# Group statistics of an attention block by VectorE transposes in place of matmuls, one early input block, and a new load order

## The chip, the cores and the metric

The kernel runs on one core of a Trainium2 chip. The metric is the time of one execution on the device in microseconds (us). Several executions are timed, and the median is given with the lowest and the highest. An execution over 1.5% above the fastest of its kernel would count as slow and none was: over all calls the kernel before runs from 1662.96 to 1671.88 us, 0.5% apart (the two single looks, at the kernel before and at the last experiment, count as unknown), and all ratios come from rounds in which the kernel before ran on the same chip.

## The reference

```python
def reference(x, gn_scale, gn_bias, qkv_w, qkv_b, proj_w, proj_b):   # x: (4, 512, 48, 48) f32
    hn = group_norm(x, 32 groups) * gn_scale + gn_bias     # mean and var over 16 channels x 48 x 48
    qkv = einsum('oc,bchw->bohw', qkv_w, hn) + qkv_b       # 1536 x 512
    q, k, v = split(qkv as float16, 8 heads of 64)
    w = softmax((q * s)^T (k * s))                         # 2304 x 2304 for each head and batch
    a = (w v^T) as float32
    return x + einsum('oc,bchw->bohw', proj_w, a) + proj_b
```

The group norm is the part that was changed. A group is 16 neighbouring channels, and channels lie on partitions, so the mean and the variance of a group are sums over 16 partitions. Everything else (three projections, scores, exponentials, values, output projection) is unchanged.

## The kernel before

The 512 channels are 4 chunks (`c`) of 128 partitions; the 2304 positions are 5 blocks (`j`) of 512, 512, 512, 512 and 256. Each batch is 4 pairs of heads (`g`) by 5 blocks, so attention runs through 80 blocks in all. The kernel issues scores and values of one unit after another and puts the projections ("beside" work: q and k as `pqk`, v as `pv`, the output as `pr`) between them, so that TensorE is filled while ScalarE computes exponentials. A block of 512 is six units, one of 256 three; a unit with nothing beside it is called bare. The sums of a softmax row (`sums`) go out and come back by DMA; their inverses come back the same way (`ib`), and GpSimd multiplies by them (the "division", `att`), checks that the sums lie within limits (`in`, `fine`) and converts the attention output to f32 for the output projection (`a`). At a hand-over the next batch's x is loaded, its statistics are taken, and the output projection of the batch before is done.

Statistics and coefficients, with the sum over 16 partitions as a matmul with a constant matrix `gmat2`:

```python
    def group_mean(b, bank, chunks=ALL):
        ...
        nc.tensor.matmul(pm, gmat2, mv[:, :, 0], start=True, stop=True)
        nc.vector.tensor_copy(mean, pm)
        nc.vector.tensor_tensor(dev, mv[:, :, 0], mean, ALU.subtract)
        nc.vector.tensor_tensor(dev2, dev, dev, ALU.mult)
        nc.vector.tensor_tensor(var, mv[:, :, 1], dev2, ALU.add)

    def group_rstd(b, bank, chunks=ALL):
        ...
        nc.tensor.matmul(pv, gmat2, var, start=True, stop=True)
        nc.vector.tensor_scalar(veps, pv, EPS, None, ALU.add)
        nc.gpsimd.tensor_tensor(rstd, veps, mhalf[:, : len(chunks)], ALU.pow)

    def coefficients(b, chunks=ALL):
        ...
        nc.vector.tensor_tensor(ga, rstd, gsc[:, cs], ALU.mult)
        nc.vector.tensor_tensor(mga, mean, ga, ALU.mult)
        nc.vector.tensor_tensor(gb, gbi[:, cs], mga, ALU.subtract)
```

The order at the start, and the residual loads, which the argument below turns on:

```python
    all_stats(0); group_mean(0, ..., (0,)); group_rstd(0, ..., (0,)); all_stats(1)
    for c in range(NC):
        coefficients(0, (c,))
        norm_chunk(0, c)                      # on ScalarE
        if c + 2 < NC: all_stats(c + 2)
        ...                                   # six projections of chunk c; mean and rstd of c + 1 between them
    # (cut) the output projection: x is loaded a second time as the residual r, one tile ahead
        for k, (jj, chunks) in enumerate(proj_list):
            ...
                [piece(0.0, lambda k=k: ahead(k)) for k in ([0] if k == 0 else [])]
                + [piece(0.0, lambda k=k: ahead(k + 1))]
                + ...
```

The first residual tile of a batch is thus loaded when its first output chain is issued, and not sooner. It goes through the same queue of SyncE as the x blocks of the next batch, behind what stands there before it: in the trace of the changed kernel shown below, x loads are issued at 1058.35, the `ib` loads at 1062.01 after a wait of 1.7 us, and the residual at 1063.17.

## Time and profile before

| | before |
|---|---|
| time, median of the first 3 executions | 1666.96 us (1666.34 to 1669.79) |
| span of the profiled execution | 1659.0 us |
| TensorE busy | 1597.6 us, 96% |
| VectorE, ScalarE, GpSimd busy | 68%, 75%, 22% |

The prediction below shows the busy table, the slices, the start and the first hand-over. Beside them stands the table by stretches, here for the three hand-overs and the last batch (columns: stretch; its length; busy time of TensorE, of its weight loads, of VectorE, ScalarE and GpSimd, each with a count; mean granted TensorE clock; DMA share; GB/s):

```profile
250.00:400.00 150.00, 140.68 (x1110) 61.57 (x1108) 120.73 (x149) 122.62 (x130) 36.82 (x41) 0.99 0.17 45
600.00:800.00 200.00, 193.98 (x1424) 93.62 (x1421) 152.02 (x184) 152.88 (x162) 55.20 (x71) 0.99 0.28 80
1000.00:1200.00 200.00, 193.69 (x1436) 92.97 (x1434) 152.04 (x184) 150.85 (x159) 51.17 (x70) 1.00 0.29 81
1400.00:1600.00 200.00, 190.90 (x1328) 88.38 (x1325) 138.28 (x139) 162.82 (x173) 63.34 (x80) 1.00 0.26 75
```

Length less the first busy number is TensorE's idle time: 9.3, 6.0, 6.3 and 9.1 us. Two waits of the output projection, in the table of waits (total us, times, longest us), come back later:

```profile
PE pr L819 <- POOL a L813: 10.8, 13, 1.5
...
PE pr L819 <- DVE r L839: 3.3, 3, 2.7
```

"pr for a" is the wait for GpSimd's conversion of the attention output to f32. "pr for r" is the wait for a free PSUM bank, which VectorE empties by adding the residual r; when r has not landed, VectorE stands and so does TensorE.

### The profile page before, as it was taken

Reading aid. Unit: us, or ns where it says so; the run is one execution under the profiler, and the core shown is the slowest. Engines: PE = TensorE matmul, PEld = TensorE weight load, DVE = VectorE, ACT = ScalarE, POOL = GpSimd, SP = SyncE. Lnnn points to the kernel's source line nnn. Section 1 sums busy time; section 2 is a strip of 40 time slices with the busy share of each in tenths; the row PEclk is TensorE's granted clock in tenths of the full one; section 3 lists DMA queues with packets and bytes.
Section 4 is the critical chain, followed back from the end, with each engine's and each line's share of the span. In section 5 each row is a group of like instructions: output and inputs, shape, how many; then the busy total and the mean of one; then the engine's idle time right before and its main releaser. Section 6 shows DMA issues by size and latency. Waiting matters only on the chain.

```text
span 1659.0 us, 28335 instructions
## 1 busy us (share of the span) xinstructions
PE 1597.6 (96%) x11528; PEld 699.7 (42%) x11528; DVE 1131.3 (68%) x1282; ACT 1246.5 (75%) x1317; POOL 370.8 (22%) x499
## 2 busy tenths in 40 slices
PE   6999999899999999999999999999999999999987
PEld 2533444244333443445433344345533334434445
DVE  4257667887666667878666666887766677676664
ACT  3078788887878877777778777876778888887772
POOL 1002112222121213232111121223111222214241
PEclk9999999999999999999999999999999999999999
DMA  6000002200000002540100000443110000003443
GB/s 215 1 1 23 15 15 65 74 14 17 14 11 14 18 14 60 161 133 17 33 14 11 14 14 11 130 119 112 24 26 11 14 17 15 15 11 124 134 126 120
DMA packets 95184, 82.10 MB, mean 49 GB/s; under 512 B 51140, under 2 KB 61252, under 8 KB 95044
## 3 DMA queue, kind: packets, MB, share of 16 engines
q1 hardware_dynamic: 93572, 79.14, 17.0%
q8 instruction: 92, 1.51, 0.4%
q10 hardware_dynamic: 1344, 1.05, 0.2%
q14 instruction: 48, 0.39, 0.1%
q0 software_dynamic: 128, 0.01, 0.0%
HBM read 60.70 MB, written 19.17 MB: 48 GB/s over the span
## 4 chain that ended last, share of the span: by engine, by line
PE 87%; DVE 4%; DMA 3%; POOL 3%; ACT 2%; issue 1%; SPq 0%; ACTq 0%; DVEq 0%; POOLq 0%
PE pqk L696 28%; PE ps L892 17%; PE av L917 17%; PE pv L741 15%; PE pr L819 7%; POOL a L813 2%; ACT p L899 2%; DVE acc L950 2%; PE ps L696 1%; PE sl L970 1%; DMA row<-inv 1%; DVE acc L953 1%; DMA ib<-row 1%; DMA out_dram<-r 1%; DVE st L605 0%
## 5 line engine op out<-in xcount | busy, mean ns | idle before, releaser
L899 ACT ACTIVATE p<-ps 128x1024 f16<-128x1024 f32 x1296 | 1231.6, 1027 | 360.9 <-PE ps L892 358.4
L950 DVE TENSOR_TENSOR acc<-acc,p 128x3072 f16<-128x3072 f16 x270 | 486.4, 1802 | 69.7 <-ACT p L899 69.0
L696 PE MATMUL pqk<-x,wqkv 128*64 128x512 f32 (+1 forms) x2464 | 518.6, 551 | 0.5 <-DVE k L705 0.4
L892 PE MATMUL ps<-q,k 64*128 64x512 f16 (+1 forms) x2880 | 362.3, 358 | 17.0 <-ACT p L899 14.9
L917 PE MATMUL av<-p,v 128*64 128x512 f16 (+1 forms) x2880 | 361.3, 364 | 0.0
L1008 POOL TENSOR_SCALAR in<-sums 128x8 f32<-128x8 f32 (+1 forms) x160 | 109.7, 686 | 726.3 <-DMA sums<-slx 719.5
L741 PE MATMUL pv<-wqkv,x 128*64 128x256 f32 x2304 | 268.1, 380 | 0.0
L696 PEld LDWEIGHTS pqk<-x,wqkv 128*64 128x64 f32 x2464 | 168.7, 137 | 226.5 <-issue 170.6
L1034 POOL TENSOR_TENSOR att<-avx,ib 128x512 f16<-128x512 f32 (+1 forms) x78 | 132.8, 1703 | 447.0 <-DMA ib<-row 366.1
L892 PEld LDWEIGHTS <-k 64*128 64x128 f16 x2880 | 107.3, 94 | 294.9 <-issue 248.2
L917 PEld LDWEIGHTS <-v 128*64 128x64 f16 x2880 | 131.7, 109 | 209.8 <-issue 165.8
L741 PEld LDWEIGHTS pv<-wqkv,x 128*64 128x64 f32 x2304 | 160.7, 137 | 92.1 <-DVE v L749 5.4
L819 PE MATMUL pr<-a,whi 128*128 128x512 f32 (+1 forms) x320 | 126.5, 403 | 14.0 <-POOL a L813 10.8
L950 DVE TENSOR_TENSOR acc<-p,p 128x3072 f16<-128x3072 f16 x79 | 139.1, 1760 | 0.0
L819 PE MATMUL pr<-a,wlo 128*128 128x512 f32 (+1 forms) x320 | 117.3, 375 | 0.0
L953 DVE TENSOR_TENSOR acc<-acc 128x1024 f16<-128x1024 f16 x156 | 113.3, 726 | 5.3
L705 DVE TENSOR_SCALAR q<-pqk,bqkv 128x512 f16<-128x512 f32 (+1 forms) x79 | 54.9, 695 | 84.2 <-PE pqk L696 83.7
L749 DVE TENSOR_TENSOR v<-pv,bv 128x512 f16<-128x512 f32 x72 | 49.8, 691 | 89.2 <-PE pv L741 88.6
L705 DVE TENSOR_SCALAR k<-pqk,bqkv 128x512 f16<-128x512 f32 (+1 forms) x75 | 52.2, 696 | 80.9 <-PE pqk L696 80.8
L839 DVE SCALAR_TENSOR_TENSOR r<-pr,bproj,r 128x512 f32<-128x512 f32 (+1 forms) x80 | 54.7, 693 | 63.4 <-PE pr L819 56.2
L926 DVE COPY avx<-av 128x512 f32<-128x512 f32 (+1 forms) x80 | 51.0, 637 | 68.6 <-PE av L917 68.4
L819 PEld LDWEIGHTS pr<-a,whi 128*128 128x128 f32 x320 | 60.5, 189 | 56.5 <-POOL a L813 22.6
(61 smaller groups left out, 467.7 us busy)
## 6 DMA issues: line engine op xcount, KB each, us to landing
r<-x_dram SPq DMA_DIRECT2D x72, 256.0 KB, 2.9
out_dram<-r SPq DMA_DIRECT2D x72, 256.0 KB, 3.0
ib<-row SPq DMA_DIRECT2D x126, 128.0 KB, 3.0
x<-x_dram SPq DMA_DIRECT2D x62, 256.0 KB, 4.5
x<-x_dram SPq DMA_DIRECT2D x16, 128.0 KB, 4.7
sums<-slx SPq DMA_DIRECT2D x128, 2.0 KB, 2.1
ib<-row SPq DMA_DIRECT2D x30, 64.0 KB, 2.8
wqkv<-qkv_wT_dram SPq DMA_DIRECT2D x2, 768.0 KB, 6.9
```

Source lines behind the costliest of these rows:

```text
L696: nc.tensor.matmul(pw[0][lo : lo + D, :n], wqkv[:, c, w0 + lo : w0 + lo + D], hn[b, c, j], start=(c == 0), stop=(c == NC - 1),)
L705: nc.vector.tensor_scalar(qk[g][part][:, o : o + n], pw[0][:, :n], bqkv[:, col : col + 1], SCALE, ALU.add, ALU.mult,)
L741: nc.tensor.matmul(pw[0][lo : lo + D, a, :], hn[b, c, i * P // QB][:, at + lo : at + lo + D], wqkv[:, c, 2 * C + half * C // 2 :][:, : C / ...
L819: nc.tensor.matmul(ps[:, :n], w[:, c, bass.ts(m, P)], at32[b, j][c], start=(c == 0 and i == 0), stop=(c == NC - 1 and i == 1),)
L839: nc.vector.scalar_tensor_tensor(xt[:, i], places[i], bproj[:, m : m + 1], xt[:, i], ALU.add, ALU.add)
L892: nc.tensor.matmul(ps[:, h, a * n : (a + 1) * n], kt[rows, bass.ts(i, P)], qt[rows, o : o + n], start=True, stop=True,)
L899: nc.scalar.activation(pt[:, r], ps, AF.Exp)
L917: nc.tensor.matmul(av[0][lo : lo + D, :n], vv[b, pr // 2][:, i, pr % 2 * P + lo : pr % 2 * P + lo + D], pt[:, r, h, a * n : (a + 1) * n], ...
L950: nc.vector.tensor_tensor(t, before, pt, ALU.add)
L953: nc.vector.tensor_tensor(t[:, 0], t[:, 0], t[:, r], ALU.add)
L1008: nc.gpsimd.tensor_scalar(t, sm, limit, None, op)
L1034: nc.gpsimd.tensor_tensor(atts[g][:, o : o + n], avx.pop((g, j))[:, :n], ibs.pop((g, j))[:, :n], ALU.mult,)
```

## The change

The intent is to take the statistics off TensorE: a VectorE transpose (0.31 us for 128x96 f32 in the trace of the changed kernel), which its code uses by squares of 32x32 with a correct result, turns the per-partition moments so that the 16 channels of a group lie along one row, one aggregation per group merges them, and a second transpose turns the coefficients back. With no round trip over TensorE, coefficients come sooner at the start and at hand-overs. The converted attention output, one tile `a32` so far, becomes four, one for each chunk. One block of the second batch's x is loaded early into buffers that the first batch does not use, and some projections are held back to fill the first hand-over. At the start x is loaded ahead of the k weights. (Cut to its core.)

```diff
-    load_w(1, slice(0, P), nc.scalar)
     for c in range(NC):
         for j in range(NQ):
             load_x(0, j, c, nc.scalar if c == 0 and j % 2 else nc.sync)
         if c == 0:
+            load_w(1, slice(0, P), nc.scalar)
             load_w(0, slice(0, P), nc.scalar)
...
-        nc.tensor.matmul(pm, gmat2, mv[:, :, 0], start=True, stop=True)      # group_mean, group_rstd gone
+    def group_scale(b, chunks=ALL):
+        turned = small_tile(SQ * 3, "turned")
+        nc.vector.transpose(turned.rearrange("p (c s) -> p s c", s=3), moments)
+        grouped = small_tile(NGROUP * 2, "grouped").rearrange("p (g s) -> p g s", s=2)
+        for i in range(NGROUP):
+            nc.vector.bn_aggr(grouped[:, i, :], turned[:, bass.ts(i, GROUP * 3)])
+        veps = small_tile(NGROUP, "veps")
+        nc.vector.tensor_scalar(veps, grouped[:, :, 1], EPS, None, ALU.add)
+        rstd = small_tile(NGROUP, "rstd")
+        nc.gpsimd.tensor_tensor(rstd, veps, mhalf, ALU.pow)
+        ...                                      # copy the means into `both`
     def coefficients(b, chunks=ALL):
+        ...                                      # copy rstd into `both`
+        nc.vector.transpose(cols, both)
...
+    SPARE = (1, 3)                               # batch 1, block 3
+        if (b, j) == SPARE:
+            t = work.tile([P, n], F32, tag=f"a32_{c}", bufs=1, name=name)
...
-                t = work.tile([P, NC, QB], F32R, tag="a32", bufs=1, name=f"a32_{b}_{j}")
+                at32[b, j] = [work.tile([P, QB], F32R, tag=f"a32_{c}", bufs=1, ...)[:, :n]
+                              for c in range(NC)]
...
+                tasks.append((now[0] + 3, lambda: aggregate(b)))   # then group_scale, coefficients,
+                tasks.append((now[0] + 3, lambda: group_scale(b))) # normalize, one after the other
...
+            put_run(reload, *SPARE)              # the early block; v tiles and q, k of block 3 held back
...
     for c in range(NC):
+        for j in range(NQ):
+            if j == 2:
+                coefficients(0, (c,)); norm_chunk(0, c)
+            if c + 1 < NC:
+                stats(0, j, c + 1)
```

More of the change, by code (lines that the diff above doesn't have):

```diff
@@ L497, in fast_path @@
     hn = {}
+    SPARE = (1, 3)
     def load_x(b, j, c, engine):
         o, n = QBLOCKS[j]
-        t = xpool.tile([P, n], F32, tag=f"x{c}_{j}", name=f"x_{b}_{c}_{j}")
+        name = f"x_{b}_{c}_{j}"
+        if (b, j) == SPARE:
+            t = work.tile([P, n], F32, tag=f"a32_{c}", bufs=1, name=name)
+        else:
+            t = xpool.tile([P, n], F32, tag=f"x{c}_{j}", name=name)
         engine.dma_start(t, x[b, bass.ts(c, P), o : o + n])
@@ L559, in split_wproj @@
         )
-    gmat = const.tile([P, P // GROUP, GROUP], F32, name="gmat")
-    nc.gpsimd.memset(gmat, 1.0 / GROUP)
-    for sign, base in ((1, 0), (-1, GROUP - 1)):
-        nc.gpsimd.affine_select(
-            out=gmat,
-            in_=gmat,
-            compare_op=ALU.is_ge,
-            fill=0.0,
-            base=base,
-            pattern=[[-sign * GROUP, P // GROUP], [0, GROUP]],
-            channel_multiplier=sign,
-        )
-    gmat2 = gmat.rearrange("p g j -> p (g j)")
-    mhalf = const.tile([P, NC], F32, name="mhalf")
+    mhalf = const.tile([P, 2], F32, name="mhalf")
     nc.gpsimd.memset(mhalf, -0.5)
@@ L592, in chain_bank @@
         return ps_w.tile([P, QB], F32, tag="pw", name=name)
-    stat, coef = {}, {}
+    stat, coef, ab = {}, {}, {}
     ALL = range(NC)
+    SQ = 32
+    NGROUP = SQ // GROUP
+    moments = const.tile([P, 3, SQ], F32, name="moments")
+    nc.gpsimd.memset(moments, 1.0)
     def stats(b, j, c):
         if b not in stat:
-            stat[b] = (
-                small.tile([P, NC, NQ, 6], F32, tag="st", bufs=1, name=f"st_{b}"),
-                small.tile([P, NC, 2], F32, tag="mv", name=f"mv_{b}"),
-            )
-        nc.vector.bn_stats(stat[b][0][:, c, j, :], hn[b, c, j])
@@ L607, in aggregate @@
-    def aggregate(b, chunks=ALL):
-        st, mv = stat[b]
-        for c in chunks:
-            nc.vector.bn_aggr(mv[:, c, :], st[:, c].rearrange("p j s -> p (j s)"))
-    def columns(b, chunks, *names):
-        for n in names:
-            if (n, b) not in coef:
-                coef[n, b] = small.tile([P, NC], F32, tag=n, name=f"{n}_{b}")
-        return [coef[n, b][:, chunks[0] : chunks[-1] + 1] for n in names]
-    def group_mean(b, bank, chunks=ALL):
-        mv = stat[b][1][:, chunks[0] : chunks[-1] + 1]
-        pm = bank[:, : len(chunks)]
-        mean, dev, dev2, var = columns(b, chunks, "gmean", "gdev", "gdev2", "gvar")
-        nc.tensor.matmul(pm, gmat2, mv[:, :, 0], start=True, stop=True)
-        nc.vector.tensor_copy(mean, pm)
-        nc.vector.tensor_tensor(dev, mv[:, :, 0], mean, ALU.subtract)
-        nc.vector.tensor_tensor(dev2, dev, dev, ALU.mult)
-        nc.vector.tensor_tensor(var, mv[:, :, 1], dev2, ALU.add)
@@ L628, in group_rstd @@
-    def group_rstd(b, bank, chunks=ALL):
-        pv = bank[:, : len(chunks)]
-        veps, rstd, var = columns(b, chunks, "veps", "rstd", "gvar")
-        nc.tensor.matmul(pv, gmat2, var, start=True, stop=True)
-        nc.vector.tensor_scalar(veps, pv, EPS, None, ALU.add)
-        nc.gpsimd.tensor_tensor(rstd, veps, mhalf[:, : len(chunks)], ALU.pow)
-    def coefficients(b, chunks=ALL):
+            stat[b] = small.tile([P, NC, NQ, 6], F32, tag="st", bufs=1, name=f"st_{b}")
+        nc.vector.bn_stats(stat[b][:, c, j, :], hn[b, c, j])
@@ new lines, in aggregate, with small_tile @@
+    def aggregate(b, chunks=ALL):
+        for c in chunks:
+            nc.vector.bn_aggr(
+                moments[:, 1:, c], stat[b][:, c].rearrange("p j s -> p (j s)")
+            )
+    def small_tile(n, tag):
+        return small.tile([P, n], F32, tag=tag, bufs=1, name=tag)
+    def group_scale(b, chunks=ALL):
+        turned = small_tile(SQ * 3, "turned")
+        nc.vector.transpose(
+            turned.rearrange("p (c s) -> p s c", s=3), moments
+        )
+        grouped = small_tile(NGROUP * 2, "grouped").rearrange("p (g s) -> p g s", s=2)
[5 more added lines that the diff above has]
+        nc.gpsimd.tensor_tensor(rstd, veps, mhalf, ALU.pow)
+        both = small_tile(SQ * 2, "both").rearrange("p (s c) -> p s c", s=2)
+        spread = both.rearrange("p s (g j) -> p s g j", g=NGROUP)
+        nc.vector.tensor_copy(
+            spread[:, 0], grouped[:, :, 0:1].to_broadcast((P, NGROUP, GROUP))
+        )
+        coef[b, chunks[0]] = both, spread, rstd
@@ L636, in coefficients @@
+    def coefficients(b, chunks=ALL):
+        both, spread, rstd = coef.pop((b, chunks[0]))
+        nc.vector.tensor_copy(
+            spread[:, 1], rstd.unsqueeze(2).to_broadcast((P, NGROUP, GROUP))
+        )
+        cols = small_tile(SQ * 2, "cols").rearrange("p (s c) -> p s c", s=2)
+        nc.vector.transpose(cols, both)
         cs = slice(chunks[0], chunks[-1] + 1)
-        ga, mga, gb, rstd, mean = columns(
-            b, chunks, "ga", "mga", "gb", "rstd", "gmean"
-        )
-        nc.vector.tensor_tensor(ga, rstd, gsc[:, cs], ALU.mult)
@@ L641, in coefficients @@
-        nc.vector.tensor_tensor(mga, mean, ga, ALU.mult)
+        ga, mga, gb = (
+            small.tile([P, NC], F32, tag=f"{n}{chunks[0] % 2}", name=f"{n}_{b}")[:, cs]
+            for n in ("ga", "mga", "gb")
+        )
+        nc.vector.tensor_tensor(ga, cols[:, 1, cs], gsc[:, cs], ALU.mult)
+        nc.vector.tensor_tensor(mga, cols[:, 0, cs], ga, ALU.mult)
         nc.vector.tensor_tensor(gb, gbi[:, cs], mga, ALU.subtract)
+        for i, c in enumerate(chunks):
+            ab[b, c] = ga[:, i : i + 1], gb[:, i : i + 1]
@@ L644, in norm @@
     def norm(b, j, c):
         t = hn[b, c, j]
-        ga, gb = columns(b, (c,), "ga", "gb")
+        ga, gb = ab[b, c]
         nc.vector.tensor_scalar(t, t, ga, gb, ALU.mult, ALU.add)
     def norm_chunk(b, c):
-        ga, gb = columns(b, (c,), "ga", "gb")
+        ga, gb = ab[b, c]
         for j in range(NQ):
@@ L762, in fast_path @@
     tasks, loads = deque(), deque()
-    normed, turn = {}, {}
+    normed = {}
     atts, res, at32 = {}, {}, {}
@@ L806, in att32 @@
             else:
-                t = work.tile(
-                    [P, NC, QB], F32R, tag="a32", bufs=1, name=f"a32_{b}_{j}"
-                )
-                at32[b, j] = [t[:, c, :n] for c in range(NC)]
+                at32[b, j] = [
+                    work.tile(
+                        [P, QB], F32R, tag=f"a32_{c}", bufs=1, name=f"a32_{b}_{j}_{c}"
+                    )[:, :n]
+                    for c in range(NC)
+                ]
         for c in pairs:
@@ L1060, in run, with normalize @@
             if j == NQ - 1:
-                tasks.append((now[0] + 3, lambda: step(aggregate, b)))
-        loads.append((now[0] + 1, run))
-    def step(run, b, *args):
-        run(b, *args)
-        turn[run, b] = now[0]
-    def follows(run, b):
-        return lambda: turn.get((run, b), now[0]) < now[0]
-    def norm_bank(b):
-        return ps_s.tile([P, 2, QB], F32, tag="ps", name=f"norm_{b}")[:, 0, :]
-    def group_scale(b):
-        group_rstd(b, norm_bank(b))
-        tasks.append((now[0] + 1, lambda: coefficients(b)))
-        for j in range(NQ):
-            for c in range(NC):
-                def run(j=j, c=c):
-                    norm(b, j, c)
-                    normed[b, j, c] = now[0]
-                tasks.append((now[0] + 1, run))
+                tasks.append((now[0] + 3, lambda: aggregate(b)))
+                tasks.append((now[0] + 3, lambda: group_scale(b)))
+                tasks.append((now[0] + 3, lambda: coefficients(b)))
+                for jj in range(NQ):
+                    for c in range(NC):
+                        tasks.append((now[0] + 3, lambda jj=jj, c=c: normalize(b, jj, c)))
+        loads.append((now[0] + 1, run))
+    def normalize(b, j, c):
+        norm(b, j, c)
+        normed[b, j, c] = now[0]
     def do_tasks(room):
@@ L1099, in put_qk, with put_v @@
             put(qk_chain(g, part, j), (g - 2) * per_pair - 1, g)
-    def put_v(b, half):
-        for i in range(0, NT, 2):
+    def put_v(b, half, tiles=range(0, NT, 2)):
+        for i in tiles:
             g = b * NPAIR + 2 * half
@@ L1139, in fast_path @@
                 put_qk(g + 1, 0, (j,))
+            put_run(reload, *SPARE)
         put_qk(g + 2, 1)
         put_qk(g + 2, 0)
-        put_v(b, 1)
+        late = SPARE[1] if b == 0 else None
+        last_tiles = [i for i in range(0, NT, 2) if i * P // QB == late]
+        put_v(b, 1, [i for i in range(0, NT, 2) if i not in last_tiles])
         if b == B - 1:
@@ L1163, in fast_path @@
         for j in range(NQ):
+            if j == late:
+                continue
             if j == 3 and b > 0:
@@ L1168, in fast_path @@
             put_run(reload, b + 1, j)
-        norms = [
-            (
-                lambda b=b: step(group_mean, b + 1, norm_bank(b + 1)),
-                follows(aggregate, b + 1),
-            ),
-            (lambda b=b: group_scale(b + 1), follows(group_mean, b + 1)),
-        ]
+        if late is not None:
+            put_v(b, 1, last_tiles)
+            put_qk(g + 3, 1, (late,))
+            put_qk(g + 3, 0, (late,))
         if b > 0:
-            for j in range(3):
+            for j in range(NQ - 1):
                 put_proj(old, j)
                 put_convert(old, j + 1)
-            put_proj(old, 3, 0)
-            put_run(norms[0][0], when=norms[0][1])
-            put_proj(old, 3, 1)
-            put_run(norms[1][0], when=norms[1][1])
-            put_proj(old, 3, 2, 3)
-            put_convert(old, 4)
-        else:
-            for run, when in norms:
-                put_run(run, when=when)
         put_v(b + 1, 0)
         if b > 0:
-            put_proj(old, 4)
+            put_proj(old, NQ - 1)
         put_qk(g + 4, 1)
@@ L1208, in all_stats @@
         aggregate(0, (c,))
-    def small_bank(name):
-        return ps_w.tile([P, QB], F32, tag="pw", name=name)
     all_stats(0)
-    group_mean(0, small_bank("mean_0"), (0,))
-    group_rstd(0, small_bank("var_0"), (0,))
-    all_stats(1)
+    group_scale(0, (0,))
     for c in range(NC):
-        coefficients(0, (c,))
-        norm_chunk(0, c)
-        if c + 2 < NC:
-            all_stats(c + 2)
-        for i, chain in enumerate(chains):
+        for j in range(NQ):
+            if j == 2:
+                coefficients(0, (c,))
+                norm_chunk(0, c)
+            if c + 1 < NC:
+                stats(0, j, c + 1)
+        if c + 1 < NC:
+            aggregate(0, (c + 1,))
+            group_scale(0, (c + 1,))
+        for chain in chains:
             chain(c)
-            if c + 1 < NC and i == 0:
-                group_mean(0, small_bank(f"mean_0_{c + 1}"), (c + 1,))
-            if c + 1 < NC and i == 2:
-                group_rstd(0, small_bank(f"var_0_{c + 1}"), (c + 1,))
     for j in range(1, NQ):
```

## The prediction

> **What bounds the kernel now.** I read the busy table first: TensorE is busy 96% of the span, everything else 75% or less, so only a change that removes TensorE idle time or TensorE work can shorten it. The 40 slices then say where the 4% idle lies: slice 1 (6 tenths), slice 8, and the last two.
>
> ```profile
> span 1659.0 us, 28335 instructions
> ...
> PE 1597.6 (96%) x11528; PEld 699.7 (42%) x11528; DVE 1131.3 (68%) x1282; ACT 1246.5 (75%) x1317; POOL 370.8 (22%) x499
> ...
> PE   6999999899999999999999999999999999999987
> ```
>
> Slices of 41 us blur short gaps, so I asked for the busy time in stretches: 25.1 of the first 41.5 us, 140.7 of 250 to 400, 194.0 of 600 to 800, 193.7 of 1000 to 1200, 190.9 of 1400 to 1600, 46.3 of the last 59. Whole stretches between them are at 100%. So there are five holes besides the tail: the start, one at each of the three hand-overs to the next batch, one in the last batch. The timeline shows what each waits for. The start (columns: start, length, engine, line, operation, idle before it and who ended that):
>
> ```profile
> 8.68 0.29 DVE L610 BATCH_NORM_AGGREGATE mv<-st 128x2 f32<-128x30 f32 x1
> ...
> 11.20 2.79 DVE L605 BATCH_NORM_STATS2 st<-x 128x6 f32<-128x512 f32 x5
> ...
> 14.56 0.16 DVE L642 TENSOR_TENSOR gb<-gbi,mga 128x1 f32<-128x1 f32 x1
> ...
> 15.63 1.98 PE L696 MATMUL ps<-x,wqkv 128*64 128x512 f32 x4 [4.54 <-ACT x L654]
> ...
> 18.05 3.68 PE L696 MATMUL ps<-x,wqkv 128*64 128x512 f32 x8
> ...
> 22.14 3.47 PE L696 MATMUL ps<-x,wqkv 128*64 128x512 f32 x16
> ```
>
> The statistics of chunk 0 are complete at 8.97, yet the coefficient gb comes at 14.72: two round trips over TensorE (mean, variance), then five statistics of chunk 1 queued ahead of the three coefficient operations. The first hand-over:
>
> ```profile
> 322.66 0.64 PE L970 MATMUL sl<-acc,ones 128*64 128x512 f16 x2 [2.07 <-DVE avx L926]
> ...
> 330.62 0.39 PE L622 MATMUL norm<-mv,gmat 128*128 128x4 f32 x2
> ...
> 333.38 0.39 PE L631 MATMUL norm<-gvar,gmat 128*128 128x4 f32 x2
> ...
> 341.03 0.41 PE L970 MATMUL sl<-acc,ones 128*64 128x512 f16 x2 [2.09 <-DVE avx L926]
> ...
> 342.12 3.67 PE L741 MATMUL pv<-wqkv,x 128*64 128x256 f32 x32
> ```
>
> From 314.9 to 342.1 there is no projection work (pqk, pv, pr) between scores and values: nine attention units run alone, because all projections of batch 0 are used up and those of batch 1 wait for its last x block, its statistics and its coefficients. One unit is three scores bursts of 0.39 us less overlap and one values burst, about 1.66 us of TensorE; nine of them and three row-sum bursts make some 16.1 us in a stretch of 27.3. So 11 us are lost there. VectorE is busy 24.8 of the 27.3.
>
> [...] 0.46 to 0.50 us per matmul at 15.63 and 18.05, 0.22 from 22.14. [...] the PEclk row shows nothing of it. [...] the power operation on GpSimd takes 0.58 us in the start but up to 2.56 beside the 1.75 us adds[...].
>
> **The change, part by part.**
> (a) Start. Removed: eight tiny f32 matmuls (0.5 us each cold, 0.3 warm) and eight waits between engines. Added per chunk on VectorE: two transposes (0.4), two aggregations (0.29 each by the row of the 128x30 one), two copies (0.14 each); dropped: gmean, gdev, gdev2, gvar (0.62). VectorE per chunk: five statistics 2.79, aggregation 0.29, transposes 0.4, aggregations 0.58, veps 0.16, copies 0.28, three coefficients 0.5, sum 5.0 us. TensorE needs 5.5 parts of 0.86 = 4.7 us a chunk, and is behind by one cold chunk, so VectorE does not bind. First coefficients: x before weights brings 256 KB forward at some 0.36 MB/us, 0.7 us; aggregation ends at 8.2, transpose 8.4, two aggregations 9.0, veps 9.2, two statistics of chunk 1 in which the power hides 10.6, then copy, transpose and three operations 11.5. ACT and the first matmul followed gb by 0.95, so TensorE starts at about 12.5 in place of 15.63: 3.1 us. Chunk 0 loses two cold matmul pairs (8.9 to 8.0 us), chunks 1 and 2 go from 5.88 us to 4.8. Chunk 3, which waits for evacuations at L705, stays. Sum **6 us**.
> (b) First hand-over. Block 3 of batch 1 gets its own buffers (those of a), so it loads some 25 units early; v tiles 12 and 14 and the q and k chains of block 3 are held back, 13.8 us of TensorE work. In the order of instructions nine bare units become three (59 to 61). But VectorE: between the row sums of units 56 and 62 its queue holds six adds (1.7), a tail of 1.4, five statistics, four aggregations, transposes and coefficients (about 3), five norms (0.5), copies and evacuations: 18.6 us, against TensorE work of 12.9. So I don't count the naive 8 us: the loss goes from 11.2 to 5.7, **5.5 us**.
> (c) Second and third hand-over. The mean and variance matmuls go (0.39 each, two pairs' worth 0.8 us per hand-over), and with them the scores bank they borrowed: waits of 0.26 (gmean) and 1.25 (veps) at 727 and 732, and the one bare unit each (184, 295), about 1 us. Second: **3 us**.
> (d) One tile a32 becomes four, so the conversion for the next block starts when chunk 0 has been read rather than when all are; the last six matmuls after chunk 0's take 1.4 us. Waits of pr for a of this kind: 1.34 and 1.32 in the third hand-over, 0.73, 1.32, 0.45, 1.37 in the last batch. Third hand-over with its 0.8: **3.3 us**; last batch **2.5 us**.
> Sum 6 + 5.5 + 3 + 3.3 + 2.5 = 20.3. I take off 2 for VectorE's queue being longer at the hand-overs by 1 us each. 1667 - 18.5 gives 1648.
>
> **Rivals.**
> First, VectorE becomes the bound at the hand-overs: the coefficients follow the aggregation at once, so VectorE stands still for the power on GpSimd (up to 2.5 us, and in the third hand-over it is queued behind four conversions). For it: 24.8 of 27.3 us busy there now. Against it: elsewhere it has a third of its time free. It would take 4 to 6 us of the gain: 1653.
> Second, the gain of the start does not come: the data, not the chain, sets the pace (DMA is at 0.9 and more from 2 to 24 us), and chunk 1's first blocks or the weights moved behind x arrive later than TensorE wants. Against it: in the kernel before statistics of chunks 1 to 3 wait for no DMA. It would cost 3 us: 1651.
> Third, the naive reading: bare units 9 to 3 at 1.2 us each plus all waits on a vanish, 26 us: 1641.
> Fourth, the change is hidden and nothing moves. Against it: TensorE is the bound before and after each hole, so a filled hole shifts everything after it.
>
> **Range and chances.** Smallest sum: start 5, hand-over 3, the rest 2, so 1657; largest 1641, and a little more for an easier VectorE: 1639. Faster by over 2% needs 33 us, which even the third rival doesn't reach.
>
> **What would show it.** Right: first matmul near 12.5, pqk starting near 38 instead of 44.4; bare stretch of three units with TensorE idle some 5 us; no gmat matmuls; waits of pr for a under half of 10.8 us. Wrong: first matmul still after 15; a wait of VectorE for rstd over 2 us at a hand-over; VectorE behind by more than a unit so that sl waits for avx longer than 2.1; the 2.69 us wait at 681 (pr for r, whose residual load is queued behind x loads) growing, since that load order is the same.

## The result, and the profile after

The changed kernel is correct. Its time is **1653.49 us** (median of 4, 1652.06 to 1657.17) against 1666.65 (1665.02 to 1669.79) for the kernel before on the same chip. The ratio is 0.9922, with a 95% interval of 0.99 to 0.9944; it is the mean time of one kernel's fast runs over that of the other's of the same rounds, so it is not quite the ratio of the medians. The change is faster by 0.8%, inside the 2% band. It gained 13.2 us where 18.5 were predicted; 1653.5 lies in the predicted range.

The page's first line and its busy line, changed kernel:

```profile
span 1652.5 us, 28302 instructions
...
PE 1591.0 (96%) x11500; PEld 695.2 (42%) x11500; DVE 1137.5 (69%) x1296; ACT 1247.7 (76%) x1317; POOL 372.1 (23%) x497
```

TensorE still bounds: its busy time fell by 6.6 us and VectorE's rose by 6.2. The profiled execution of the kernel before happened to be a quick one, so I use two profiled executions of each kernel below: spans 1659.0 and 1666.4 before, 1652.5 and 1654.8 after.

The start (timeline of the changed kernel):

```profile
8.05 0.31 DVE L617 STREAM_TRANSPOSE turned<-moments 128x96 f32<-128x96 f32 x1
8.39 0.60 DVE L622 BATCH_NORM_AGGREGATE grouped<-turned 128x2 f32<-128x48 f32 x2
...
11.65 0.16 DVE L648 TENSOR_TENSOR gb<-gbi,mga 128x1 f32<-128x1 f32 x1
...
12.71 1.12 PE L704 MATMUL ps<-x,wqkv 128*64 128x512 f32 x2 [12.71 <-ACT x L662]
```

The coefficient gb comes at 11.65 in place of 14.56 and the first matmul at 12.71 in place of 15.63. The stretches of the changed kernel (columns as above):

```profile
250.00:400.00 150.00, 144.22 (x1152) 63.43 (x1150) 115.66 (x149) 118.83 (x126) 31.99 (x41) 1.00 0.11 29
600.00:800.00 200.00, 192.68 (x1390) 90.37 (x1388) 156.29 (x190) 154.54 (x164) 59.46 (x71) 1.00 0.29 84
1000.00:1200.00 200.00, 190.60 (x1362) 90.89 (x1358) 150.34 (x185) 148.55 (x157) 57.58 (x71) 0.98 0.30 84
1400.00:1600.00 200.00, 186.56 (x1266) 85.57 (x1264) 137.39 (x138) 158.28 (x167) 62.92 (x81) 0.99 0.28 80
```

Idle time falls from 9.3 to 5.8 us in the first hand-over, rises from 6.0 to 7.3 in the second and from 6.3 to 9.4 in the third, and from 9.1 to 13.4 in the last. The clock of 0.98 in the third is time at half speed: the granted clock was 0.50 from 1069 to 1072 us and from 1100 to 1103, and 1.00 from 1073 to 1080. The last stretch can't be compared by its window, because the changed kernel is some 12 us further on in it; the table below takes it from a block on. I count as the loss of a stretch its idle time plus (1 less the clock) times its length, taken in steps of 10 us. As means of two executions each:

| | before | after |
|---|---|---|
| projections of the first unit start at | 44.5 us | 36.9 us |
| loss, 250 to 400 us | 12.0 | 6.5 |
| loss, 600 to 800 us | 8.6 | 6.8 |
| loss, 1000 to 1200 us | 6.7 | **12.9** |
| from the 71st of 80 attention blocks to the end | 197.9 | **201.4** |

By the 61st block, behind all three hand-overs, the changed kernel is 12.7 us ahead (by the start of VectorE's 61st copy of the summed values, means of two). In the last batch it gives 3.6 back. From the 71st block on TensorE's idle time is 22.6 us before and 23.5 after, the half-clock loss 3.7 and 6.1 (means of two, from 2.7 and 4.6 to 3.3 and 8.9). So most of what is given back is time at half clock, which varies from execution to execution.

TensorE's order in the last batch is also not the same. The changed kernel runs a bare unit at 1502.19, where the kernel before goes on with an output chain (1511.96); the kernel before has its bare unit at 1547.98. In between every output chain of the changed kernel stands one unit later against the attention. With it goes a longer wait in SyncE's queue: a residual load has to wait until an earlier output has been stored and its buffer is free, in all 56.2 us in 22 waits from 1440 us on, against 36.1 in 16 before (59.8 and 38.0 in the second traces). What stands behind it is late. In the changed kernel the row sums are ready at 1530.65 and issued at 1534.87, checks and conversion follow, and the output chain waits 2.26 us; in the kernel before such sums are ready at 1543.91 and issued at 1543.94. (The first three lines are the changed kernel.)

```profile
1534.43 0.34 SPq L799 DMA_DIRECT2D r<-x_dram  x1
1534.87 1.14 SPq L994 DMA_DIRECT2D sums<-slx  x2
...
1540.84 0.50 PE L829 MATMUL pr<-a,whi 128*128 128x512 f32 x1 [2.26 <-POOL a L823]
```

```profile
1543.94 1.15 SPq L984 DMA_DIRECT2D sums<-slx  x2
```

This is read from the traces; no run changes it alone.

The table of waits of the changed kernel names the third hand-over's loss:

```profile
PE pr L829 <- DVE r L849: 11.3, 8, 5.2
...
PE pr L829 <- POOL a L823: 8.7, 11, 2.3
```

pr for r has grown from 3.3 to 11.3 us, with one wait of 5.2. The timeline around it (SPq is SyncE's queue of DMA issues, in order):

```profile
1058.35 1.84 SPq L510 DMA_DIRECT2D x<-x_dram  x4
...
1060.41 0.50 PE L829 MATMUL pr<-a,whi 128*128 128x512 f32 x1
...
1062.01 1.12 SPq L1037 DMA_DIRECT2D ib<-row  x2
1063.17 1.05 SPq L799 DMA_DIRECT2D r<-x_dram  x2
...
1068.42 0.75 DVE L849 SCALAR_TENSOR_TENSOR r<-pr,bproj,r 128x512 f32<-128x512 f32 x1 [6.07 <-DMA r<-x_dram]
...
1069.23 0.79 PE L829 MATMUL pr<-a,whi 128*128 128x512 f32 x1 [5.17 <-DVE r L849]
1069.82 0.63 PE L829 MATMUL pr<-a,wlo 128*128 128x512 f32 x1
```

SyncE issues four x loads, then stands 1.7 us for the row that `ib` reads, and only then issues the residual, 2.8 us after TensorE has begun the chain that needs it. VectorE stands 6.07 us for r, TensorE 5.17, and the matmuls then run at 0.63 us, where 0.40 is usual, until the granted clock goes from 0.50 (1069 to 1072) back to 1.00 (from 1073). In the kernel before, same place:

```profile
1073.97 1.19 SPq L791 DMA_DIRECT2D r<-x_dram  x2
...
1083.59 0.74 DVE L839 SCALAR_TENSOR_TENSOR r<-pr,bproj,r 128x512 f32<-128x512 f32 x1
```

There r is issued 7.2 us before the chain starts (its first matmul is at 1081.18) and 9.6 before it is read, and nobody waits. The residual's code is the same in both kernels. What differs is where TensorE's projection falls against that queue.

### The profile page after: what moved, and what is told of

Same layout as the page of the kernel before. It is cut to its first block, busy times and chain, and to the rows that moved or that the text cites. A ratio compares the mean times of both kernels' runs of the same rounds, so it can differ in the third digit from the quotient of the medians.

```text
span 1652.5 us, 28302 instructions
## 1 busy us (share of the span) xinstructions
PE 1591.0 (96%) x11500; PEld 695.2 (42%) x11500; DVE 1137.5 (69%) x1296; ACT 1247.7 (76%) x1317; POOL 372.1 (23%) x497
## 4 chain that ended last, share of the span: by engine, by line
PE 86%; DMA 5%; DVE 4%; POOL 2%; issue 2%; ACT 1%; SPq 1%; DVEq 0%; POOLq 0%
PE pqk L704 28%; PE ps L902 17%; PE av L927 17%; PE pv L749 15%; PE pr L829 6%; DMA out_dram<-r 2%; DVE acc L960 1%; PE ps L704 1%; PE sl L980 1%; POOL a L823 1%; DMA r<-x_dram 1%; ACT p L909 1%; DMA ib<-row 1%; DMA x<-x_dram 1%; DMA sums<-slx 1%
## 5 line engine op out<-in xcount | busy, mean ns | idle before, releaser
L902 PE MATMUL ps<-q,k 64*128 64x512 f16 (+1 forms) x2880 | 360.7, 359 | 10.8 <-ACT p L909 10.4
L1018 POOL TENSOR_SCALAR in<-sums 128x8 f32<-128x8 f32 (+1 forms) x160 | 121.3, 758 | 716.0 <-DMA sums<-slx 709.3
L829 PE MATMUL pr<-a,whi 128*128 128x512 f32 (+1 forms) x320 | 127.2, 405 | 23.1 <-DVE r L849 11.3
```

Source lines behind the costliest of these rows:

```text
L829: nc.tensor.matmul(ps[:, :n], w[:, c, bass.ts(m, P)], at32[b, j][c], start=(c == 0 and i == 0), stop=(c == NC - 1 and i == 1),)
L902: nc.tensor.matmul(ps[:, h, a * n : (a + 1) * n], kt[rows, bass.ts(i, P)], qt[rows, o : o + n], start=True, stop=True,)
L1018: nc.gpsimd.tensor_scalar(t, sm, limit, None, op)
```

## The experiments

Twelve runs were made. Repeats come first, because they show how far a difference can be read.

**The two kernels again.**

> The kernel before once more, unchanged, for a second trace. Its first trace (span 1659.0 us) was 6 us shorter than the median of its timed runs (1666.65). Theory: the waits of a hand-over for the residual x (pr for r, 2.69 us at 681 us in the first trace) vary from run to run, and this trace shows a span of 1660 to 1668 us with the difference in TensorE idle time at the second or third hand-over; the start (pqk from 44.4 us) and the first hand-over (pv from 342.1 us) repeat within 0.5 us. Rival: the difference lies in the start or in the clock, so pqk starts over 1 us later than 44.4.

> The kernel after once more, unchanged, as a base on this chip for the other runs: 1652 to 1657 us, ratio to before 0.990 to 0.994. Theory: its trace shows the long waits of pr for r (5.17 us at 1069 us in the first trace) again within 2 us, because the order of the DMA queue makes them. Rival: chance; the wait at the third hand-over is under 2 us this time and another place has it.

The kernel before: 1668.22 us (one look). The changed kernel: 1655.13 us (1653.84 to 1656.56), ratio 0.9928 (0.9911 to 0.9945). The wait of pr for r at the third hand-over stands in the second trace too (5.47 us, at 1068.01); it belongs to the kernel and not to one execution. The second trace of the kernel before has a span of 1666.4 and repeats the start and the first hand-over within 0.5 us, as expected (44.53 and 342.50). But the 7.4 us by which the spans differ are not mainly idle time, as the theory had it: 5.1 of them are half-clock time in the four stretches.

**Residual loads early.** The first two residual tiles of a batch are loaded with the batch's first conversion, ahead of the x loads that stood before them.

```diff
-                [piece(0.0, lambda k=k: ahead(k)) for k in ([0] if k == 0 else [])]
-                + [piece(0.0, lambda k=k: ahead(k + 1))]
+                [piece(0.0, lambda k=k: ahead(k + 1)) for k in ([] if k == 0 else [k])]
...
+        if j == 0:
+            for k in range(2):
+                put_run(residual, b, *proj_list[k])
         put(projs[b, j][0], end + ready(b, j))
```

> After, with the first two residual loads of a batch moved in the DMA queue: from the unit of the first output projection, behind the x loads of the next batch and behind an ib load that waits for its row, to the first conversion, ahead of the last two x blocks. Theory (the second and third hand-over gave the expected gain back to late residual loads): pr waits for r 11.3 us fall below 5, the 5.17 us wait at the third hand-over is gone, 4 to 8 us faster than after, 1646 to 1650 us. Rival (VectorE's longer queue and the power on GpSimd made the loss): within 2 us of after, and pr then waits for something else as long.

Measured: **1646.26 us** (1645.18 to 1650.47), ratio 0.9885 (0.9864 to 0.9907), 8.9 us under the changed kernel of the same call. Its table of stretches and of waits:

```profile
1000.00:1200.00 200.00, 195.89 (x1407) 91.21 (x1402) 156.80 (x191) 155.09 (x164) 57.58 (x71) 1.00 0.30 84
```

```profile
PE pr L829 <- DVE r L849: 5.1, 7, 1.4
```

The loss of the third hand-over falls from 12.9 to 4.1 us, about the 8.9 that the time shows, and no wait for r is longer than 1.4. So the third hand-over lost its gain to the residual in SyncE's queue: shown.

**The same edit on the kernel before.**

> The kernel before with the residual loads early alone. Theory: in the kernel before the residual's late arrival cost only 2.7 to 3.3 us of TensorE wait (pr for r, at 681 above all) and nothing at the third hand-over, so it gains 1 to 3 us: 1664 to 1666; the 8.9 us that early residuals gave the changed kernel are then mostly repair of a wait that the change itself enlarged. Rival: early residuals are worth the same 8 to 9 us in any kernel: 1658.

Measured: 1663.98 us (1660.27 to 1667.0, 12 executions), ratio 0.9988 (0.9979 to 0.9998): 3.2 us by the medians, 2.0 by the ratio. The kernel before had no such wait in the third hand-over, so early residuals repair what the change itself brought about.

**Without the early x block.** `SPARE` is set to a block that does not exist, so that nothing is preloaded or held back.

```diff
-    SPARE = (1, 3)
+    SPARE = (-1, -1)
-            put_run(reload, *SPARE)
-        late = SPARE[1] if b == 0 else None
+        late = None
```

> After without the spare block: block 3 of the second batch is loaded in its old place and nothing is held back; statistics, start and the four conversion tiles stay. The order of instructions has seven bare attention units at the first hand-over (66 to 72) in place of three. Theory (VectorE fills most of the three units, so four units fewer are worth less than 1.2 us each): 4 to 6 us slower than after, 1657 to 1660 us. Rival, the naive count: seven bare units cost what nine cost before, 11 us, against 3.3 for three: 8 us slower, 1661 or more. Second rival: the preload is worth nothing, since statistics without matmuls end the bare stretch anyhow: within 2 us of after.

Measured: 1655.78 us (1652.92 to 1656.6), ratio 0.9936 (0.992 to 0.9953), the same as the changed kernel (1655.13). Taken alone this reads as "the block is worth nothing". The stretches say otherwise: the first hand-over loses 12.1 us in place of 6.5, but the third loses 2.6 in place of 12.9, because the shifted schedule misses the late residual by chance. Hence the same edit with early residuals:

> Residual loads early, and no spare block: compare with e_res_early (1646.3). Theory: the spare block is worth what the trace shows at the first hand-over, 5 to 6 us (TensorE idle and half-clock loss from 250 to 400 us 12 in e_no_spare against 6 to 7 with the block), and e_no_spare equalled the changed kernel only because its shifted schedule missed the late residual block at the third hand-over. Then this run is at 1651 to 1652.5. Rival: the spare block is worth nothing, the holes that it fills open later: then within 1.5 us of e_res_early, 1645 to 1648.

Measured: 1656.89 us (1655.15 to 1657.25), ratio 0.9938 (0.9917 to 0.9958), 10.6 above the early residuals with the block; I had expected 5 to 6. The first hand-over loses 12.2 against 5.5 us, as expected, and the second 11.2 against 6.5, which I had not. Its timeline there:

```profile
697.27 1.26 POOL L1043 TENSOR_TENSOR att<-avx,ib 128x512 f16<-128x512 f32 x1 [8.18 <-DMA ib<-row]
698.49 0.72 POOL L626 TENSOR_TENSOR rstd<-veps,mhalf 128x2 f32<-128x2 f32 x1
...
699.25 0.57 DVE L636 COPY both<-rstd 128x32 f32<-128x32 f32 x1 [3.48 <-POOL rstd L626]
...
702.27 0.77 PE L829 MATMUL pr<-a,whi 128*128 128x512 f32 x1 [5.58 <-DVE r L849]
```

GpSimd took its queue in order here: the power's inputs were written by 695.68, and it started at 698.49, as the division before it ended. That division had waited 8.18 us for a DMA. VectorE stands 3.48 us for the power because the coefficients are next in its own queue, the additions that free PSUM stand behind that, and TensorE waits 5.58. This is the prediction's first rival, seen whole, though in this variant; in the changed kernel VectorE waits at most 0.79 us for the power.

**The power later.** From the third batch's statistics on, the power is issued one unit later, behind the conversion copies, and the coefficients one unit after it. (Variants with the power on VectorE were also meant; no such run is on record, and nothing here rests on them.)

```diff
-                tasks.append((now[0] + 3, lambda: group_scale(b)))
-                tasks.append((now[0] + 3, lambda: coefficients(b)))
+                def scale_and_coefficients():
+                    power = group_scale(b)       # issues the power itself where b < 2
+                    wait = 0 if b < 2 else 1
+                    tasks.appendleft((now[0] + 2 * wait, lambda: coefficients(b)))
+                    if b >= 2:
+                        tasks.appendleft((now[0] + wait, power))
+                tasks.append((now[0] + 3, scale_and_coefficients))
```

> Residual loads early, and from the third batch's statistics on the power is put into GpSimd's queue one unit later, behind the conversion copies, the coefficients one unit after that. Compare with e_res_early (1646.3). Theory: at the second hand-over the conversion of the first projection block is late by the power's wait for VectorE's veps (GpSimd idle 3.9 us until 677.9), which TensorE shows as a 2.7 us wait of pr near 681; with the power behind the copies that wait and the half-clock spell after it go: 2.5 to 4 us, so 1642.5 to 1644. Rival: the wait is from the residual or from VectorE's add of 1.75 us and stays: 1645 to 1648 and pr still waits over 2 us near 681.

> The same kernel as e_res_pow once more, on another call. e_pow_sums_dve and e_pow_coef_late came out 7 to 8 us above it, while their traces explain 2 to 4 us by the edits (the rest lies in stretches that the edits do not touch: 3.4 us already at 1091, before the first changed instruction of e_pow_sums_dve). If e_res_pow's 1643.7 belongs to the kernel: 1642.5 to 1645 again, and the edits cost what their times say. If it is the chip or the call: 1646 to 1650, and small differences between calls are not to be read.

Measured: **1643.65 us** (1642.81 to 1644.84), ratio 0.9861 (0.9841 to 0.9882); in another call, on another chip, 1648.33 us (1645.74 to 1650.6), ratio 0.9892 (0.9876 to 0.9909). With early residuals alone, the second hand-over had looked like this:

```profile
677.47 0.72 POOL L626 TENSOR_TENSOR rstd<-veps,mhalf 128x2 f32<-128x2 f32 x1 [3.88 <-DVE both L629]
678.14 3.80 POOL L823 CAST a<-att 128x512 fp32r<-128x512 f16 x4
...
680.31 0.80 PE L829 MATMUL pr<-a,whi 128*128 128x512 f32 x1 [2.71 <-DVE both L636]
```

With the power later:

```profile
674.30 2.96 POOL L829 CAST a<-att 128x512 fp32r<-128x512 f16 x4 [1.15 <-PE pr L835]
...
684.90 1.17 POOL L628 TENSOR_TENSOR rstd<-veps,mhalf 128x2 f32<-128x2 f32 x1
```

The copies start at 674.30 in place of 678.14, and the 2.71 us wait is gone from both traces: GpSimd had idled 3.88 us for VectorE's veps with four copies behind it. (The line names VectorE's copy L636 as the releaser; the first copy of a ended within 0.05 us of it, and the weight load of the same chain waited 3.2 us for a. That first copy took 2.12 us beside VectorE's addition of 1.75, the other three 0.61 each, so the power's place is not the whole of the delay.) But four or five waits for r of 0.5 to 1.7 us stand there now, where there was one of 0.65, and the loss of the second hand-over only goes from 6.5 to 5.5 and 6.7 us. The wait was explained rightly, and the gain in time is not shown: the two calls of this one kernel lie 4.7 us apart, on both sides of 1646.26.

That scatter limits what follows. A difference of under 5 us between calls is not read from times here, only from the stretches of the traces.

**Power later, without the early block.**

> Residuals early and power later, without the spare block: compare with e_res_pow (1643.7). e_res_no_spare was 10.6 us above e_res_early, where 5 to 6 were expected; its trace shows 6.7 us more loss at the first hand-over and 4.7 more at the second, there a 5.6 us wait of pr near 702 while VectorE waits 3.5 us for rstd, which lies behind a division in GpSimd's queue. Theory: the spare block is worth the first part only, the second was the power's queue falling badly with another schedule: with the power later it goes, so 1649 to 1651.5. Rival: the block is worth all 10 us (the second hand-over needs it too): 1653 or more.

Measured: 1652.42 us (1651.44 to 1658.58), ratio 0.992 (0.9895 to 0.9946), between the two expectations. The first hand-over loses 11.4 us against 5.5; the second 9.0 against 5.5 and 6.7: the 5.58 wait for r is gone, and pr waits 3.99 us for a at 699.36 instead. In all three traces without the block the first hand-over loses 11.4 to 12.2 us, in those with it 5.5 to 7.6: the block is worth some 5 to 6 us there. Without it the second is worse by 2 to 5 us as well, by how the queues happen to meet.

**One joint a32 tile.** The four converted tiles are one tile again, with early residuals.

```diff
-                at32[b, j] = [work.tile([P, QB], F32R, tag=f"a32_{c}", bufs=1, ...)[:, :n] for c in range(NC)]
+                t = work.tile([P, NC, QB], F32R, tag="a32", bufs=1, name=f"a32_{b}_{j}")
+                at32[b, j] = [t[:, c, :n] for c in range(NC)]
```

> Residual loads early, with one joint converted tile a32 in place of four: the next conversion starts when all four chunks of the projection before are read. Compare with e_res_early (1646.3). Theory of the prediction (its part d): waits of pr for a on TensorE grow by some 4 us over the third hand-over and the last batch, so 1650 or more. Rival: the split hides nothing, since GpSimd's in-order queue (power, output sums, waits for row-sum transfers) delays the conversion in any case: 1645 to 1648, with the waits of pr for a at the same size within 1.5 us.

Measured: 1651.07 us (1648.77 to 1652.43), ratio 0.9905 (0.9883 to 0.9927), 4.8 above the early residuals of another call, as much as the scatter. The stretches say more: the third hand-over loses 7.7 us against 4.1; from 1440 to 1600 the losses are alike, 15.9 and 15.8. The waits of pr for a come to 10.1 us against 8.1. So, by one trace, the split is worth some 3.6 us in the third hand-over, half of it one spell at half clock that another execution may lack, and nothing that can be seen in the last batch.

**The last batch: checks of the row sums on VectorE.** In the last batch pr of the changed kernels waits 1.9 to 2.5 us for a near 1530 to 1540, where the kernel before has 1.32 at most, and 1.8 to 2.2 once more near the end, where the kernel before has 1.37 in one trace and 1.96 in the other. Near 1530 to 1540 the copies stand in GpSimd's queue behind a division and four checks.

```diff
-            nc.gpsimd.tensor_scalar(t, sm, limit, None, op)
-            nc.gpsimd.tensor_tensor(ok, ok, t, ALU.mult)
+            engine = nc.vector if g >= (B - 1) * NPAIR else nc.gpsimd
+            engine.tensor_scalar(t, sm, limit, None, op)
+            engine.tensor_tensor(ok, ok, t, ALU.mult)
```

> e_res_pow with the checks of the row sums of the last batch on VectorE in place of GpSimd. Compare with e_res_pow (1643.7). Theory: the last batch is slower than in the kernel before because the conversion copies stand in GpSimd's queue behind a division and four checks, one of 1.63 us, that wait for transfers (pr waits 2.5 us at 1527.95 for a): without the checks the copies start 1.5 to 2.5 us sooner, and the run is at 1641 to 1642.5. Rival: the conversion is late by its place in the schedule, or VectorE gets later by what GpSimd gains: 1643 to 1646.

Measured: 1651.48 us (1650.32 to 1652.35), ratio 0.9902 (0.9885 to 0.9918). It did not gain. That wait near 1535 is no longer one for a, but for r (1.65 us): VectorE now stands 2.46 us for the sums of a DMA at 1533.13 and frees PSUM late. The waits of pr for r come to 11.1 us against 6.2, and another wait for a, 2.87 us at 1483.89, has appeared. My theory of the last batch, that the checks on GpSimd are what costs, does not hold as a cure. Part of the 3 to 8 us that this kernel stands above its base lies before the first instruction that the edit touches: at the 61st block it is 4.7 and 2.2 us behind the two traces of its base. From there to the end it takes 1.5 and 2.6 us more than they do, so the edit did not gain in its own stretch either.

**The coefficients of the start behind all five statistics.**

```diff
-            if j == 2:
-                coefficients(0, (c,)); norm_chunk(0, c)
             if c + 1 < NC:
                 stats(0, j, c + 1)
+            if j == NQ - 1:
+                coefficients(0, (c,)); norm_chunk(0, c)
```

> e_res_pow with each chunk's start coefficients behind all five statistics of the next chunk, as the kernel before ordered them. One look at the start only. Theory of the prediction: three more statistics of 0.56 us stand before the first coefficients, so gb at 13.2 in place of 11.6, first matmul at 14.1 in place of 12.5, and the projections of the first unit start 1.3 to 1.7 us later (38.7 in place of 37.4). Rival: TensorE's cold matmuls, not the coefficients, set the pace: the first matmul is later but the projections start within 0.5 us of 37.4.

One look: 1650.49 us. The start in its timeline:

```profile
14.18 17.73 PE L710 MATMUL ps<-x,wqkv 128*64 128x512 f32 x76 [14.18 <-ACT x L668]
...
38.97 11.33 PE L710 MATMUL pqk<-x,wqkv 128*64 128x512 f32 x56
```

The first matmul moves from 12.52 to 14.18 and the projections from 37.04 to 38.97: the delay of the first coefficients goes through one to one. So of the 7.6 us that the start gained, 1.9 come from putting the coefficients between the statistics; the rest belongs to the transposes and to x first, which no run parts. Of it, the statistics of chunk 0 are complete at 8.01 in place of 8.97, before any transpose.

## Why the prediction was right or wrong, point by point

The time, 1653.5, was inside the range and the verdict, within 2%, was right. That it falls on the first rival's 1653 is luck: what was lost lay elsewhere than that rival said. Two small slips stand in the working: 20.3 less 2 is 18.3, not 18.5, and the stretch of nine bare units holds two bursts of row sums, not three. By steps:

- **(a) Start, 6 us: right, a little low.** The projections start 7.6 us sooner (44.5 to 36.9), the first matmul at 12.71 where 12.5 was predicted. Its 3.1 us came as 3.1 (means of two); the stream behind it gave 4.5 where 2.9 was left over for it. The transposes took 0.31 us (96 columns of f32) and 0.24 (64 columns); the 0.4 us for the two in the working was the author's estimate, and the kernel before has no transpose that shows it. "Cold" in the working stands for the slower first matmuls, 0.46 to 0.50 us each up to 22.14 in the kernel before and 0.22 from there; why they are slower is not shown, and the granted clock reads 1.00 in every stretch from 15 to 32 us. The rival that data sets the pace is refuted by the run with late coefficients: the coefficients do. Of the data, one statistic of chunk 1 waits 0.30 us for its x, at 10.17.
- **(b) First hand-over, 5.5 us: right.** The loss went from 12.0 to 6.5. VectorE is the bound in it, as the step said: v waits 2.71 us for a normalized x at 309.33. The power took 2.24 us there (from 300.37), beside an addition of 1.75 us on VectorE, and ended 0.58 us behind it, at 302.61; the other six powers of the trace took 0.69 to 0.72. In the kernel before it took 2.48 us at 1138.90 beside an addition of 1.75, 2.56 at 336.23 beside one of 2.87, and 0.55 to 0.58 in the start. Why it takes longer there is not shown. Taking the block away loses it again, in three traces.
- **(c) Second hand-over, 3 us: right in size.** The loss fell by 1.8, and 0.8 of matmul work is gone, so 2.6. The 2.72 us wait near 681 did not grow, but its cause did change: from the residual to GpSimd's queue, where the power stood ahead of the copies. That is the kind of loss that the first rival named, priced there at 4 to 6 us in all; its own sign, a wait of VectorE for rstd over 2 us, is not in the changed kernel.
- **(d) Third hand-over, 3.3 us gained: wrong, and this is the step that failed.** The loss rose by 6.2 us; with the 0.8 us of removed matmuls that is 5.4 lost. The mechanism of the step is there (the split is worth some 3.6 us by the run with one tile, and with early residuals the stretch loses 4.1, which with the 0.8 is a gain of 3.4), but the step took the order of loads against TensorE as fixed. The chain moved closer to the reload of x than its residual load could follow, and r came 5.2 us late. The prediction had named this wait as what would make it wrong, from the second hand-over, without a number. With the residual early, the kernel gives 1646.26, 20.6 us under the 1666.83 that the kernel before took in that call; the predicted sum was 20.3 before the 2 us taken off. The agreement is luck, since the last batch still loses in that run.
- **(d) Last batch, 2.5 us gained: wrong.** It lost 3.6. No gain from the split can be seen there. It removed waits of the kind that the step named (0.73 and 1.32 near 1517 and 1533 before, 0.17 after), but the longer waits for a that remain (2.26 and 1.82 in the first trace) follow conversions that start right behind checks or a division in GpSimd's queue. All waits of pr for a came to 8.7 us, 10.8 before, and not to under half as the prediction's sign had it. Why the stretch is slower is not shown. Most of the loss is half-clock time; TensorE's order differs there, and SyncE's queue stands longer for output buffers, as told above. All eight traces with the changed kernel's order in the last batch take 377.3 to 382.0 us from the 61st block to the end, one tile or four, and the three with the old order (both of the kernel before, and its early residuals) 374.0 to 377.1. Moving the checks did not mend it, and no run changed the order or the number of output buffers alone, so the cause stays open.
- **2 us off for VectorE's longer queue:** no run measures it by itself.

The sum by measurement is 7.6 + 5.5 + 2.6 - 5.4 - 3.6 = 6.7 us. The profiled spans differ by 9.1 (means of two) and the times by 13.2. Of the first difference, 0.8 is the first hand-over's removed matmuls, which no term counts; the other 1.6 is not assigned. Of the second, note that the profiled execution of the kernel before was the quickest of all of its runs here.

Whether a wait is followed by a spell at half clock changes from execution to execution: the 2.71 us wait at 680.31 with early residuals was followed by matmuls that start at 0.80 us (clock 0.84 from 680 to 690), the 2.72 us wait at 680.71 in the changed kernel by one of 0.50 as usual. With the power later, in the second call, a wait of 2.05 us at 1587.05 was followed by one of 0.79. A spell costs up to 1.7 us (clock 0.83 from 320 to 330 and from 680 to 690 in the kernel before). The kernel before had two such losses in one trace and five in the other, the changed one some three and some seven. In the kernel before they make 5.1 of the 7.4 us between its two spans; how much of the scatter between calls they are is not shown.

## What to carry to other kernels

When a change brings forward the consumer of a load, look up where that load stands in its queue and what the entries ahead of it wait for; here two early loads, worth 8.9 us, were as much as two thirds of the whole change (13.2). Look up too where an operation put on a little-used engine stands in that engine's queue, ahead of or behind what the bound engine needs next; here the power on GpSimd (23% busy in the changed kernel), behind a division that waited 8.18 us, came before a TensorE wait of 5.58 us in the run without the early block. An edit that changes nothing in the total may have gained in one stretch and lost in another, so read each stretch before calling a part worthless, and repeat a kernel in another call before reading a difference of a few us.
